# Second attention layer: the lead of a block's load and sum over its moments, and a buffer of the router's own for turned tokens

## The chip, the cores and the metric

The kernel runs on one core of a Trainium2 chip. The metric is the device time of one execution in microseconds (us). Times of the kernel before: 1226.37, 1233.04 and 1235.10 us, median 1233.04. The profile comes from one further execution.

## The reference, cut to what matters

Tokens x are 16 sequences of 256 with 128 features, 4096 tokens in all. Four residual sublayers follow each other: causal attention, a mixture of experts, a second attention with a distance-like score, and the same mixture of experts.

```python
x = x + attn_a(layernorm(x))   # 16 heads of 8, causal softmax
x = x + ffn(layernorm(x))      # 8 experts, each token goes to its best 2
x = x + attn_b(layernorm(x))   # softmax of -(|q|max^2 - 2 q k + |k|max^2) / (|q|_F * |x|_inf)
x = x + ffn(layernorm(x))      # the same weights

# ffn
logits = flat_x @ Wr
top_vals, top_idx = top_k(logits, 2);  rw = softmax(top_vals)
g = einsum('nc,ech->neh', flat_x, Wg); u = einsum('nc,ech->neh', flat_x, Wu)
eo = einsum('neh,ehc->nec', silu(g) * u, Wd) / sqrt(12)
out = sum over the two chosen experts of rw * eo
```

`layernorm` has no weights: (x - mean) / sqrt(variance + 1e-5), over the 128 features.

## The kernel before, in words

**Blocks and rounds.** The tokens are cut into 8 blocks (n = 0 to 7) of 512 tokens, which are two sequences (b = 0, 1). An attention layer runs 128 rounds, 16 for each block; each round handles two pairs of heads of one sequence. In a round PE makes scores by rows (`rows_scores`), DVE takes their maximum (`mx<-s`, `rows_maxima`), and 14 rounds later PE makes the scores of the same heads again by columns and ACT turns them into exponentials (`p<-s`). Three rounds after that PE multiplies them with the values (`av<-p,v`), and so on. Rounds of two blocks therefore overlap.

**The planner.** All other work of a layer is written as Python generators that yield between their steps `(rounds to wait, work(DVE us, ACT us, needs the PSUM bank))`. `later` (line 1306) puts a step on a list with the round from which it is due; `due` (line 1309), called twice in a round, takes the due steps in order of rank and age, as long as the DVE and ACT time stated for them fits the `room` of the round (1.7 and 1.4 us in the second layer) and the one PSUM bank `ps` (pool `mm`, one buffer) is not already claimed. `work()` without a number costs nothing in this account. The planner runs when the program is built; the engines then execute fixed queues, each in its order. All instructions of the kernel are recorded through one helper, so that nearly all show as line 250 in the profile; the names of tiles tell them apart. The scatters of the router are declared free of mutual order (`unordered`, line 471), and stand in POOL's queue earlier than the planner's round for them.

**The steps of a block.** `project(n)` (line 915) starts 15 to 17 rounds ahead of the block's own rounds in the second layer. It loads the block: in the second layer each token's value lies in DRAM as two halves, `xb` and `more` (line 898 to 913, on SP's DMA queue). Then, step by step: POOL adds the halves (line 925, `xb<-xb,more`); after a yield DVE takes the mean and variance (`moments`, line 316: `st<-xb`, `mv<-st`, two tiles of 128 tokens in one round and two in the next), POOL computes 1/sqrt and the shift (`rstd`, `shift`); ACT normalises into `xn` (line 336); PE transposes `xn` and ACT copies the result to `xnT` (`turned_block`, line 352); q and k are projected from `xnT`; scale factors are found from sums over q, k and x (`scales`, line 1050, with the small tile `den`, copied from PSUM by DVE and raised to a power by POOL); q is scaled and split into a high part by ACT and a low part by DVE (`hi`, `lo`, lines 980 to 991); the parts are laid out for the heads by DMAs on SP (`lay`, line 1019, `q<-hi`, `q<-lo`, `k<-hi`, `k<-lo`); last, the values are projected from the same `xnT` (line 994) and POOL adds a bias (`xb<-xb,extra_b`).

**The end of a block.** When a block's attention output `o` is complete, `finish(n)` (line 1272) is put on the list at line 1270: PE turns `o`, ACT copies it, PE projects it, DVE adds it to `xb`, and SP stores the sum. Then `route(n)` (line 376), the router: `moments` again, normalised rows into `both_rows` (ACT reads `xb` for the last time here, which frees the block's buffer; `blocks` has five of them, so the load of block n+5 waits for it), `turned_block` again, logits, the two best experts, the place of each token in its expert's queue, its two weights (DVE, `both_rows<-share`), and eight indirect DMAs on POOL that scatter the rows by expert (`rows_in<-both_rows,slots`).

**The experts.** Scattered rows form tiles of 256 (some of 128 in the second layer's end). A tile has four parts (`gu<-xT`, `y<-w_d,h`). One part can run in each round once tiles are known; what is left when the layer's loop ends runs alone after it (`rest`).

**Buffers.** A pool's `bufs` says how many tiles with one tag exist at a time. The attention's pool has two for each tag unless stated, and `xnT` of `project` and of `route` share one tag.

Of the kernel before, what the change touches and what calls it, by code (L numbers as in the profile page):

```python
# [45 lines left out]
F32 = mybir.dt.float32  # L46
# [8 lines left out]
P = 128  # L55
# [11 lines left out]
TB = 512  # L67
NT = TB // P
# [15 lines left out]
def work(v=0.0, s=0.0, bank=False):  # L84

    return bank, v, s
# [7 lines left out]
def layers(  # L94
# [73 lines left out]
    psum = ctx.enter_context(tc.tile_pool(name="mm", bufs=1, space=PSUM))  # L168
# [180 lines left out]
                ALU.subtract, ALU.mult,  # L349
            )  # L350

    def turned_block(pool, psum, xn, ts=range(NT)):

        ps = psum.tile([P, TB], F32, tag="mm")
        for t in ts:
            te.transpose(ps[:, bass.ts(t, P)], xn[:, t, :], ident)
        xnT = pool.tile([P, TB], F32, tag="xnT")
        some = slice(ts[0] * P, ts[-1] * P + P)
        se.copy(xnT[:, some], ps[:, some])
        return xnT  # L360
# [15 lines left out]
    def route(pool, psum, n, xb, free, mixture):  # L376

        mv, rstd, shift = yield from moments(pool, xb)  # L380
        yield 3, work(s=0.8)

        both_rows = pool.tile([P, 2, NT, W], F32, tag="both_rows", bufs=2)
        xn = both_rows[:, 0, :, 0:P]
        yield from normed_in_steps(xn, xb, rstd, shift)
        po.tensor_copy(
            both_rows[:, :, :, P],
            tokens[:, :, n * NT : (n + 1) * NT],
        )
        yield 2, work(s=0.6, bank=True)  # L390
        xnT = turned_block(pool, psum, xn)
        yield 1, work(s=0.6)
        se.copy(both_rows[:, 1, :, 0:P], xn)
        yield 1, work(0.8, bank=True)
        ps = psum.tile([P, NT, NE], F32, tag="mm")
        for t in range(NT):
            te.matmul(ps[:, t, :], lhsT=xnT[:, bass.ts(t, P)], rhs=wr_sb, start=True, stop=True)
        lg = pool.tile([P, NT, NE], F32, tag="lg")
        ve.tensor_copy(lg, ps)
        top1, one1 = yield from best(pool, lg, 1)  # L400
        yield 1, work(0.8)
        rest = pool.tile([P, NT, NE], F32, tag="rest")
        ve.scalar_tensor_tensor(rest, one1, -3.0e38, lg, ALU.mult, ALU.add)
        top2, one2 = yield from best(pool, rest, 2)
        both = chosen[n % 2]
        ve.tensor_tensor(both[:, 0:NT, :], one1, one2, ALU.add)
        share = pool.tile([P, 2, NT], F32, tag="share")
        ve.tensor_tensor(share[:, 1], top2, top1, ALU.subtract)
        yield 2, work(0.4, 0.2, True)
        se.activation(share[:, 1], share[:, 1], AF.Exp)  # L410


        ps = psum.tile([P, NT + 1, NE], F32, tag="mm")
        te.matmul(
            ps.rearrange("p t e -> p (t e)"), lhsT=before, rhs=both.rearrange("p t e -> p (t e)"),
            start=True, stop=False,
        )
        for t in range(NT):
            te.matmul(
                ps[:, t + 1 :, :], lhsT=ones_h,  # L420
                rhs=both[:, t : t + 1, :].to_broadcast([P, NT - t, NE]),
                start=False, stop=t == NT - 1,
            )
        place = pool.tile([P, NT, NE], F32, tag="place")
        ve.tensor_tensor(
            place, ps[:, 0:NT, :], free[0].unsqueeze(1).to_broadcast([P, NT, NE]), ALU.add
        )
        after = pool.tile([P, NE], F32, tag="after")
        ve.tensor_tensor(after, ps[:, NT, :], free[0], ALU.add)
        free[0] = after  # L430
        yield 1, work(0.9)
        row = pool.tile([P, 2, NT], F32, tag="row")
        for s, one in enumerate((one1, one2)):
            mine = pool.tile([P, NT, NE], F32, tag=f"mine{s}")
            ve.tensor_tensor(mine, one, place, ALU.mult)
            ve.tensor_reduce(row[:, s, :], mine, AX.X, ALU.add)
        ve.tensor_copy(slots[n], row)
        yield 1, work(0.6)

        w1, w2 = both_rows[:, 0, :, P + 1], both_rows[:, 1, :, P + 1]  # L440
        ve.tensor_scalar_add(share[:, 0], share[:, 1], 1.0)
        ve.reciprocal(share[:, 0], share[:, 0])
        ve.tensor_scalar_mul(w1, share[:, 0], DEPTH_SCALE)
        ve.tensor_tensor(w2, share[:, 1], w1, ALU.mult)
        last = n == TOKENS // TB - 1
        chosen_tiles = mixture.choose(n, free[0], last)
        if last:
            yield 1, work(0.9)
            yield from chosen_tiles
        for t in range(NT):  # L450
            for s in range(2):

                if s == 0 or not mixture.second:
                    yield 1, FREE
                scatter = po.indirect_dma_start(
                    out=rows_in,
                    out_offset=bass.IndirectOffsetOnAxis(ap=slots[n][:, s, t : t + 1], axis=0),
                    in_=both_rows[:, s, t, :], in_offset=None,
                )
                unordered(scatter, mixture.rows)  # L460
                mixture.sent.append(scatter)
                if last:
                    mixture.pad(2 * t + s)
        if not last and sure(n):
            yield 1, work(0.9)
            yield from chosen_tiles
        if sure(n):
            yield 2, FREE
            mixture.admit()
# [413 lines left out]
    def attention(w, causal, name, mixture, ahead=None):  # L883

        with ExitStack() as own:
            pool = own.enter_context(tc.tile_pool(name=f"att_{name}", bufs=2))
# [28 lines left out]
            def project(n, b0=0, nb=2):  # L915
# [4 lines left out]
                xb, ts = xs[n], range(2 * b0, 2 * (b0 + nb))  # L920
# [2 lines left out]
                yield (3, work(0.9)) if causal else (3 if n < 3 else 4, FREE)  # L923
                if not causal:
                    po.tensor_tensor(xb[:, ts[0] : ts[-1] + 1], xb[:, ts[0] : ts[-1] + 1], more, ALU.add)
                    yield 1 if n < 3 else 2, work(0.9)
                mv, rstd, shift = yield from moments(pool, xb, n < 2, ts, causal or n > 1)
                yield 3 if causal else 2, work(s=0.8)
                if causal and n == 0:
# [316 lines left out]
            def collect(n, b, f, av, o):  # L1246

                au = pool.tile([P, 2, SEQ], F32, tag="au")
                se.copy(au, av)
                yield 1, work(0.6, bank=True)  # L1250
                ps = mm[0].tile([P, 2, 2, 4, HS], F32, tag="mm")
                for t in range(2):
                    for e in range(2):
                        te.transpose(
                            ps[:, t, e, :, :].rearrange("p i r -> p (i r)"),
                            au[:, e, bass.ts(t, P)], ident,
                        )
                ps = ps.rearrange("p t e i r -> p t (e i) r")
                inv = pool.tile([P, 2, 8], F32, tag="inv")
                ve.reciprocal(inv, ps[:, :, :, 0])  # L1260
                width = 4 * HD
                ve.tensor_tensor(
                    o[:, 2 * b : 2 * b + 2, (f - 1) * width : (f + 1) * width].rearrange(
                        "p t (i r) -> p t i r", r=HD
                    ),
                    ps[:, :, :, 1 : 1 + HD],
                    inv.unsqueeze(3).to_broadcast([P, 2, 8, HD]), ALU.mult,
                )
                if b == 1 and f == NQ - 1:
                    later(2, work(s=0.6, bank=True), finish(n, outs.pop(n)))  # L1270

            def finish(n, o):
                ps = mm[0].tile([P, TB], F32, tag="mm")
                for t in range(NT):
                    te.transpose(ps[:, bass.ts(t, P)], o[:, t, :], ident)
                oT = pool.tile([P, TB], F32, tag="oT", bufs=1)
                se.copy(oT, ps)
                yield 1, work(0.7, bank=True)
                ps = mm[0].tile([P, NT, P], F32, tag="mm")
                for t in range(NT):  # L1280
                    te.matmul(
                        ps[:, t, :], lhsT=oT[:, bass.ts(t, P)], rhs=w["wo"], start=True, stop=True
                    )
                ve.tensor_tensor(xs[n], ps, xs[n], ALU.add)
                store = sy.dma_start(out=tokens_of(mixture.total, 0, n), in_=xs[n])
                unordered(store, mixture.adds)
                mixture.stores.append(store)
                yield 1, work(0.9)
                yield from route(pool, psum, n, xs.pop(n), free, mixture)
# [16 lines left out]
            def later(rounds_on, kind, task, rank=1):  # L1306
                tasks.append((at + rounds_on, kind, rank, task))
# [214 lines left out]
```

## Time and profile before

| What | Value |
|---|---|
| Runs | 1226.37, 1233.04, 1235.10 us |
| Profiled execution, its time / its span | 1236.46 / 1234.7 us |
| Mean granted TensorE clock | 0.924 |
| First layer's rounds | 24.9 to 378.4 us (first maximum to last exponential) |
| Its experts alone | about 404 to 580 us |
| Second layer's rounds | 580.9 to 1009.6 us |
| Its last routing and first tiles | to about 1091 us |
| Its experts alone, then the output | to 1206 us, to 1234.7 us |

The span runs from the first to the last instruction; the execution's own time is 1.8 us longer. Rows of a timeline give the start, the length, the engine, the operation and its tiles as out<-in; a bracket at the end tells how long the engine was idle before, and what ended that. A row of the waits names who waited for whom, the total, how often, and the longest. PE is TensorE's matrix engine and PEld its weight loads, DVE is VectorE, ACT is ScalarE, POOL is GpSimd, SP is the engine that issues most DMAs.

### The profile page before, as it was taken

The page shows a single profiled execution, that of the slowest core. Times are in us where ns is not written, and L with a number is a line of the kernel's source. Part 1 is how long each engine was busy: PE and PEld are TensorE (multiplying, and loading weights), DVE is VectorE, ACT ScalarE, POOL GpSimd, SP SyncE. Part 2 cuts the span into 40 slices and gives each one's busy share as a digit, 9 for nine tenths or more (in the row PEclk, how much of TensorE's full clock was granted, in tenths as well). Part 3 has the DMA queues.
Part 4 walks back from the last instruction along what each step waited for, and adds up shares of the span by engine and source line. Part 5 has one row for each costly group of instructions (what it writes and reads, how often), then busy time and mean ns, then how long its engine had stood idle before and what let it go on. Part 6 is the DMA issues. An engine that isn't in the chain of part 4 may idle for free. (4 is left out here: it accounts for less than half of the span.)

```text
span 1234.7 us, 24185 instructions
## 1 busy us (share of the span) xinstructions
PE 1015.7 (82%) x8128; PEld 740.9 (60%) x8128; DVE 804.8 (65%) x2289; ACT 631.3 (51%) x1331; POOL 601.7 (49%) x681
## 2 busy tenths in 40 slices
PE   5888888979988989996678788668888886889991
PEld 3455555646666879985344445435546665779980
DVE  6666887676754756665577867668687535656662
ACT  3466665535554434453246766556656663334440
POOL 5345666454576775565221220431516675555551
PEclk9899999989999999999569988888889999999996
DMA  3355433225335798775232222222243444678876
GB/s 98 85 152 151 115 89 104 79 69 166 76 96 118 184 210 196 176 193 111 69 88 75 58 70 62 80 83 71 74 134 84 108 96 125 162 186 210 219 173 212
DMA packets 185408, 151.49 MB, mean 123 GB/s; under 512 B 16322, under 2 KB 159940, under 8 KB 185284
## 3 DMA queue, kind: packets, MB, share of 16 engines
q1 hardware_dynamic: 155842, 127.18, 36.3%
q0 software_dynamic: 25552, 18.30, 10.0%
q10 hardware_dynamic: 3890, 4.46, 1.2%
q8 instruction: 65, 1.06, 0.4%
q14 instruction: 59, 0.48, 0.1%
HBM read 83.06 MB, written 32.08 MB: 93 GB/s over the span
## 5 line engine op out<-in xcount | busy, mean ns | idle before, releaser
L250 DVE TENSOR_REDUCE mx<-s 128x6 f32<-128x768 f32 (+1 forms) x256 | 276.7, 1087 | 84.9 <-PE s L250 74.7
L250 ACT ACTIVATE p<-s 128x768 f32<-128x768 f32 (+1 forms) x256 | 234.7, 917 | 170.5 <-PE s L250 155.0
L250 POOL DMA_INDIRECT total<-y,to x149 | 233.8, 1569 | 154.0 <-ACT sg L250 59.8
L250 DVE SCALAR_TENSOR_TENSOR sg<-sg,gu 128x256 f32<-128x256 f32 (+1 forms) x267 | 107.2, 401 | 148.8 <-ACT sg L250 91.8
L250 POOL DMA_INDIRECT rows_in<-both_rows,slots x128 | 127.8, 999 | 102.7 <-DVE both_rows L250 52.0
L250 PE MATMUL y<-w_d,h 128*128 128x128 f32 x1192 | 162.6, 279 | 17.4 <-ACT y L250 10.9
L250 PEld LDWEIGHTS y<-w_d,h 128*128 128x128 f32 x1192 | 156.2, 192 | 30.9 <-ACT y L250 14.3
L250 PE MATMUL gu<-xT,w_g 128*128 128x256 f32 (+1 forms) x534 | 158.9, 380 | 13.5 <-ACT xT L250 4.8
L250 ACT ACTIVATE sg<-gu 128x256 f32<-128x256 f32 (+1 forms) x267 | 98.7, 370 | 131.3 <-PE gu L250 86.0
L250 PE MATMUL gu<-xT,w_u 128*128 128x256 f32 (+1 forms) x534 | 153.9, 370 | 0.0
L250 PE MATMUL s<-k,q 62*128 62x256 f32 (+1 forms) x1024 | 137.8, 351 | 9.6 <-DVE mx L250 4.0
L250 POOL TENSOR_SCALAR_AFFINE_SELECT p<-p 128x512 f32<-128x512 f32 x128 | 88.3, 696 | 116.5 <-ACT p L250 116.0
L250 PE MATMUL s<-q,k 64*128 64x256 f32 (+1 forms) x1024 | 110.6, 296 | 30.7 <-DVE mx L250 25.6
L250 PE MATMUL av<-p,v 128*9 128x256 f32 (+1 forms) x2048 | 130.4, 374 | 0.0
L250 PEld LDWEIGHTS s<-k,q 62*128 62x128 f32 x1024 | 84.4, 204 | 74.3 <-issue 46.7
L250 PEld LDWEIGHTS s<-q,k 64*128 64x128 f32 x1024 | 83.6, 199 | 50.9 <-DVE mx L250 38.4
L250 PEld LDWEIGHTS gu<-xT,w_u 128*128 128x128 f32 x534 | 100.1, 193 | 12.5
L250 PEld LDWEIGHTS gu<-xT,w_g 128*128 128x128 f32 x534 | 87.6, 192 | 26.4 <-ACT xT L250 7.0
L250 DVE SCALAR_TENSOR_TENSOR h<-gu,sg 128x256 f32<-128x256 f32 (+1 forms) x237 | 95.8, 404 | 8.1
L250 ACT ACTIVATE y<-y,x_in 128x128 f32<-128x128 f32 x149 | 54.8, 368 | 79.1 <-PE y L250 57.5
L250 PEld LDWEIGHTS av<-p,v 128*9 128x9 f32 x2048 | 45.0, 92 | 65.5 <-issue 33.9
L250 POOL TENSOR_TENSOR lo<-to,hi 128x512 fp32r<-128x512 f32 (+1 forms) x27 | 32.3, 1195 | 78.3 <-ACT hi L250 77.1
(242 smaller groups left out, 1410.5 us busy)
## 6 DMA issues: line engine op xcount, KB each, us to landing
w_g<-in_L_ffn_Wg_dram SPq DMA_DIRECT2D x79, 256.0 KB
w_u<-in_L_ffn_Wu_dram SPq DMA_DIRECT2D x79, 256.0 KB
w_d<-in_L_ffn_Wd_dram SPq DMA_DIRECT2D x79, 256.0 KB
x_in<-rows_in SPq DMA_DIRECT2D x70, 130.0 KB
k<-hi SPq DMA_DIRECT2D x64, 128.0 KB
k<-lo SPq DMA_DIRECT2D x64, 128.0 KB
q<-hi SPq DMA_DIRECT2D x60, 128.0 KB
q<-lo SPq DMA_DIRECT2D x60, 128.0 KB
```

The costliest lines, as they stand in the source:

```text
L250: return tc.keep_in_program_order(method(*args, **kwargs))
```

## The change

Three things differ. First, in the second layer's `project`, for blocks 3 to 7, the yield between POOL's add and the moments is four rounds long, not two. Second, `turned_block` takes a tag and a number of buffers, and `route` calls it with a tag of its own, `routed`, with one buffer, so that the router's transposed tokens no longer share the two `xnT` buffers. Third, `finish` is put on the planner's list in both layers with an ACT time of 0 instead of 0.6 us; what it executes is the same.

```diff
-    def turned_block(pool, psum, xn, ts=range(NT)):
+    def turned_block(pool, psum, xn, ts=range(NT), tag="xnT", bufs=2):
...
-        xnT = pool.tile([P, TB], F32, tag="xnT")
+        xnT = pool.tile([P, TB], F32, tag=tag, bufs=bufs)
...
-        xnT = turned_block(pool, psum, xn)
+        xnT = turned_block(pool, psum, xn, tag="routed", bufs=1)
...
                     po.tensor_tensor(xb[:, ts[0] : ts[-1] + 1], xb[:, ts[0] : ts[-1] + 1], more, ALU.add)
-                    yield 1 if n < 3 else 2, work(0.9)
+                    yield 1 if n < 3 else 4, work(0.9)
...
                 if b == 1 and f == NQ - 1:
-                    later(2, work(s=0.6, bank=True), finish(n, outs.pop(n)))
+                    later(2, work(bank=True), finish(n, outs.pop(n)))
```

## The prediction, made before the changed kernel ran

> **What bounds the kernel now.** I read the page's head first, then the engines' busy time by stretch, then the second layer's waits, then a timeline where the longest wait lies, last the chain. The page:
>
> ```profile
> span 1234.7 us, 24185 instructions
> PE 1015.7 (82%) x8128; PEld 740.9 (60%) x8128; DVE 804.8 (65%) x2289; ACT 631.3 (51%) x1331; POOL 601.7 (49%) x681
> ```
>
> No engine is full over the whole. By stretch (length, then PE, PEld, DVE, ACT and POOL busy; PE clock):
>
> ```profile
> 640.00:728.00 88.00, 70.13 (x710) 39.95 (x710) 68.72 (x142) 65.41 (x116) 15.36 (x21) 0.98 0.23 64
> 728.00:832.00 104.00, 74.31 (x666) 44.24 (x658) 69.16 (x193) 59.80 (x108) 32.32 (x43) 0.86 0.26 72
> 1096.00:1205.00 109.00, 108.26 (x710) 98.35 (x708) 71.81 (x227) 50.84 (x154) 59.17 (x39) 1.00 0.80 196
> ```
>
> The last row is the second layer's expert tiles run alone: PE-bound, 99%. The two above are its attention rounds, and there PE, DVE and ACT are all under 80%: each round is a relay PE scores, DVE maximum, PE scores, ACT exponential, and a stop of one engine soon stops all. Between 728 and 832 PE drops from 80% to 71% busy. Its waits (total, times, longest, between 640 and 963):
>
> ```profile
> PE ps L250 <- DVE den L250: 18.9, 5, 7.5
> DVE st L250 <- POOL xb L250: 14.3, 3, 6.6
> POOL xb L250 <- DMA more<-total: 8.3, 1, 8.3
> SPq L250 <- ACT both_rows L250: 33.4, 3, 12.4
> ```
>
> The longest, in order of time (bracket: idle before, and what ended it):
>
> ```profile
> 820.92 0.17 DVE L250 TENSOR_TENSOR both_rows<-share,both_rows 128x4 f32<-128x4 f32 x1
> 821.18 1.08 POOL L250 DMA_INDIRECT rows_in<-both_rows,slots  x1 [17.56 <-DVE both_rows L250]
> ...
> 826.35 0.96 POOL L250 DMA_INDIRECT rows_in<-both_rows,slots  x1 [0.30 <-issue]
> 827.34 1.28 POOL L250 TENSOR_TENSOR xb<-xb,extra_b 128x512 f32<-128x512 f32 x1
> 828.56 1.27 POOL L250 TENSOR_TENSOR lo<-to,hi 128x512 fp32r<-128x512 f32 x1
> 829.78 1.26 POOL L250 TENSOR_TENSOR xb<-xb,more 128x512 f32<-128x512 f32 x1
> 831.07 0.29 DVE L250 BATCH_NORM_STATS2 st<-xb 128x6 f32<-128x128 f32 x1 [6.60 <-POOL xb L250]
> 831.97 0.15 DVE L250 COPY den<-ps 128x2 f32<-128x2 f32 x1
> 832.27 1.09 PE L250 MATMUL ps<-ident,o 128*128 128x128 f32 x4 [7.50 <-DVE den L250]
> 833.28 0.79 PE L250 MATMUL s<-k,q 62*128 62x256 f32 x4
> ```
>
> This is block 7's start. DVE finishes a router's weights at 820.92; only then POOL may start the router's scatters, which stand ahead of the block's add in POOL's queue; five scatters and two 1.3 us operations later the sum exists. DVE stood at the block's first statistic for 6.60 us; behind it waits `den<-ps`, which empties the one PSUM bank that PE's next transpose needs: PE stands for 7.50 us. Nothing works. The same picture stands at 782.97 (DVE 5.07, PE 5.98, block 6) and 730.69 (DVE 2.63, PE 3.54, block 5). Sums: DVE 14.3, PE 17.0 us.
>
> **The change part by part.** Nothing is computed that wasn't; it is a new order. I count rounds by DVE's 128 `mx<-s` of the layer.
>
> *Statistics four rounds after the add (line 926).* Block 7: before, the router's weights come in round 83 and the statistic in 85, with five scatters ahead of the add; after, 84 and 87, with six. POOL's path is then 6 x 1.26 + 1.26 = 8.8 us (1.26 is the step from one scatter to the next) against three rounds of 2.3 us (rounds 16 to 48, 642.5 to 717.4) to 3.0 us (48 to 96, to 863.5), 6.9 to 9: 0 to 1.9 us stay, I take 1.5; 5.1 go. Block 6: weights in round 67, statistic in 69 before; 61 and 71 after: all 5.07 go. The cover is POOL, free again by about round 65.
>
> Block 5's 2.63 has another cause: its load. The block takes the buffer of block 0, which the router reads in rounds 47 and 51, while the load stands in SP's queue in round 47: the SP row, 33.4 us in three waits, and POOL's 8.3 us for the landing. *`finish` with no ACT cost (line 1270)* lets the planner start it and the router sooner: the reads come in rounds 44 and 45 (blocks 6 and 7: 66/68 to 62/64 and 79/83 to 76/78, loads in 63 and 79). The 2.63 go. SP's freed time I cost at nothing: what stood behind it (scores' rows, k and q lays) was used rounds later.
>
> So DVE gets back 14.3 - 1.5 = 12.8 us. As nothing else ran, I count it whole. Is it more? After each stop DVE idles once more (2.00, 2.23, 2.00 us), while PE refills. Here a rule bears on it: the Trainium skill, "TensorE: Matmul & The Clock Gate", Part 1, halves the clock after an idle window of about 3.4 us and wants another of that length of work to restore it. The row agrees in kind (four `s` in 0.79 us after the stop, 0.50 at 822.28), not in size: by the rule three stops cost 3 x 3.4 / 2 = 5.1 us more; by the trace, 0.3 us per four matmuls and part of 6.2 us of idle. I take 2.
>
> *What comes later instead.* All later steps of a block move by four to five rounds, its q lay (four DMAs on SP) too: scaled in rounds 46, 61, 77, 93, 108 for blocks 3 to 7 (before 41, 57, 73, 89, 104), first used in 48, 64, 80, 96, 112. Rows for block 4:
>
> ```profile
> 759.37 1.22 DVE L250 TENSOR_REDUCE mx<-s 128x4 f32<-128x1024 f32 x1
> 763.13 0.50 PE L250 MATMUL s<-q,k 64*128 64x256 f32 x4 [0.23 <-DVE mx L250]
> ```
>
> These are round 61's maximum and round 64's scores. Scaled after it (0.89 us for the two `lo`), q is ready at 761.5; two issues and a landing follow. The DMA records of this trace give 2.0 us from the last issue to the last packet (issue 752.34, end 754.41), so q lands at 764.2, 1.1 us late; DVE's round-64 maximum began only at 766.14, so little is seen. Block 3 has two rounds: maximum at 713.11, q at 715.2, landed 717.9, scores wanted at about 715.4: 2.5 us. Behind PE's wait stand the values' matmuls and, by the bank, DVE. I take 2.5 + 3 x 0.5 = 4 us; between 0 (hidden) and 5 x 4 = 20 (landing as slow as the 7.26 us of the chain's `t<-total`).
>
> *The buffer of its own (lines 352, 391).* Needed since block n+1's turned tokens may now come before block n's are read out. No wait for an `xnT` buffer stands in the trace: 0, either way.
>
> *More tiles inside.* Routers end sooner (block 0's last scatter in round 65 instead of 71), so the layer's expert work starts in round 113 instead of 116: 68 parts instead of 64 lie inside the rounds, the loop has one turn more, and one tile less stays for the end. The chain prices a tile there:
>
> ```profile
> 1096.34 2.59 PE gu L250 x12
> 1101.80 2.59 PE gu L250 x12
> ```
>
> 5.5 us. The extra turn costs 2.4 (the last 34 run from 1009.6 to about 1091), the three parts in rounds 113 to 115 between 0 and 3 x 1.4; I take 1. Net -2.
>
> *The first layer* is reshuffled by the same `finish` line. Its turns (180) and parts inside (72) stay. A rule speaks here against counting on any order: the skill's "SBUF — State Buffer", "SBUF: two separate sides", says that GpSimd and a VectorE operation with two SBUF inputs lock each other out for whole instructions. The trace has it once dearly: `m<-mx`, usually 0.2 us, takes 4.98 at 255.20 beside four POOL operations, and PE idles 5.88 us. By the rule a new order can lift or repeat it: -5 to +5. By the rows, a dozen others cost 0.8 to 1.0 each: nearer 0, which I take.
>
> Sum: -12.8 - 2 + 4 - 2 + 0 = -13. The profiled execution took 1236.46 us (span 1234.7 and 1.8 around it), 3.4 over the median of 1233.04; -13 on either, so 1220 on the median's scale.
>
> **The rivals.**
> - *The stop moves* (0.24). One bank (`ps`), and a DVE in order, make any late operand a stop: six scatters before block 7's add, or another POOL operation behind them. For: POOL still gets scatters in runs of six. Against: blocks 5 and 6 have ten rounds of room. Half the gain, with q's 4: 1233 - 6.5 + 3, or less: 1226 to 1236.
> - *q comes late for every block* (0.14), the slower side. Place: PE at the first scores of blocks 3 to 7; it decides once q lands over two rounds, about 6 us, after the lo. At 6 us late for five blocks, 30 less the 17 gained otherwise, +13: 1246. For: SP also carries k's lay of the block's other half in the same round, four DMAs of 0.6 us. Against: 2.0 us landings in this stretch at 23 to 27% DMA share.
> - *More comes* (0.12): cold clock at the rule's 5 us, the 4.98 us lock gone, block 7's 1.5 too: 1209.
> - *Forecast* (0.50): 1213 to 1226.
>
> **How the numbers follow.** 1% is about what a measurement can tell from no change: 1220.7 and 1245.4. Faster by more: all of the 0.12 and about 0.29 of the forecast's 0.50, 0.41. Within 1%: 0.21 and 0.24, 0.45. Slower: 0.14. The range, 1207 to 1238, leaves out the late q and some of the best case.
>
> **What would show it.** DVE's waits for POOL's `xb` in the attention rounds under 4 us in all, PE's for `den` under 4; no SP wait for `both_rows` over 5 us; POOL's `xb` without a wait for `more`. A row "PE s <- DMA q" tells of late q: up to 4 us expected. The final tiles alone should take 5.5 us less. I am wrong if DVE's statistics run free and the layer's rounds still take as long, or if PE waits for q by more than 10 us.

## The result, and the profile after

The changed kernel takes 1239.15 us (median of 16 runs, 1233.45 to 1247.48) against 1232.32 us for the kernel before (16 runs): ratio 1.006, interval 1.0036 to 1.0084. Forecast was 1220 us. A few executions were slow ones, at a lower clock (two of seven in `three_rounds_blocks67`, at most two of 22 in the other runs): medians in this document are of all executions, ratios of the rest. The profiled execution took 1241.53 us, span 1239.7. Two lines of its page:

```profile
span 1239.7 us, 24203 instructions
PE 1033.8 (83%) x8128; PEld 752.7 (61%) x8128; DVE 797.4 (64%) x2286; ACT 635.4 (51%) x1334; POOL 602.4 (49%) x684
```

PE issues the same 8128 matmuls and is busy 18.1 us longer (1015.7 before). The same stretches as before the change, and the last expert tiles alone (length, then PE, PEld, DVE, ACT and POOL busy, PE clock, DMA share, GB/s):

```profile
640.00:728.00 88.00, 72.38 (x718) 42.04 (x716) 66.23 (x142) 64.08 (x114) 15.90 (x23) 0.94 0.25 68
728.00:832.00 104.00, 83.33 (x714) 48.11 (x706) 74.08 (x194) 62.79 (x113) 29.07 (x40) 0.84 0.25 70
1101.00:1210.00 109.00, 108.02 (x705) 97.92 (x705) 71.22 (x226) 50.00 (x151) 58.87 (x38) 1.00 0.83 202
```

Between 728 and 832 us PE now runs 80% of the time, not 71%, and 714 matmul records lie there instead of 666: this stretch did become faster. But the clock fell in both, from 0.98 to 0.94 and from 0.86 to 0.84. The waits of the rounds (640 to 975 us; total, times, longest):

```profile
POOL xb L250 <- DMA more<-total: 33.3, 3, 14.3
DVE mx L250 <- PE s L250: 31.6, 31, 4.0
DVE sg L250 <- ACT half_g L250: 13.0, 7, 4.9
ACT sg L250 <- POOL h L250: 4.2, 1, 4.2
PE s L250 <- DMA q<-lo: 1.8, 1, 1.8
PE ps L250 <- DVE den L250: 1.8, 2, 1.2
```

DVE's wait for POOL's sum (14.3 us) is gone from the list, PE's for `den` has fallen from 18.9 to 1.8, SP's for `both_rows` is gone too. POOL's wait for `more`, which was to go, grew from 8.3 to 33.3 us; no statistic of DVE waits behind it. What has grown is `mx` waiting for PE's scores (22.7 before) and DVE's `sg` waiting for `half_g` (5.1 before). Block 7's start, in order of time, shows how well the stop was removed:

```profile
830.33 1.27 POOL L250 TENSOR_TENSOR xb<-xb,more 128x512 f32<-128x512 f32 x1
831.54 1.27 POOL L250 TENSOR_TENSOR lo<-to,hi 128x512 fp32r<-128x512 f32 x1
832.98 0.98 POOL L250 DMA_INDIRECT rows_in<-both_rows,slots  x1 [0.17 <-issue]
...
833.46 0.29 DVE L250 BATCH_NORM_STATS2 st<-xb 128x6 f32<-128x128 f32 x1
```

Block 7's statistic begins at 833.46, in round 87 as the prediction had it, without a bracket: the sum (first line) had been ready for 1.86 us. In one profiled execution of each kernel, measured from one block's first maximum to the next one's, the stretches of 16 rounds went: rounds 48 to 95 together from 146.1 to 148.8 us although the three stops lay there, 96 to 111 from 51.5 to 57.4, 112 to 127 from 48.3 to 58.4; from the last maximum to the end 271.5 became 262.1.

### The profile page after: what moved, and what is told of

The parts are those of the page before. It is cut to its first block, busy times and chain, and to the rows that moved or that the text cites. A ratio compares the mean times of both kernels' runs of the same rounds, so it can differ in the third digit from the quotient of the medians.

```text
span 1239.7 us, 24203 instructions
## 1 busy us (share of the span) xinstructions
PE 1033.8 (83%) x8128; PEld 752.7 (61%) x8128; DVE 797.4 (64%) x2286; ACT 635.4 (51%) x1334; POOL 602.4 (49%) x684
## 5 line engine op out<-in xcount | busy, mean ns | idle before, releaser
L250 POOL DMA_INDIRECT total<-y,to x149 | 233.8, 1569 | 142.8 <-ACT sg L250 64.9
L250 POOL TENSOR_SCALAR_AFFINE_SELECT p<-p 128x512 f32<-128x512 f32 x128 | 85.5, 670 | 119.4 <-ACT p L250 118.4
L250 PE MATMUL av<-p,v 128*9 128x256 f32 (+1 forms) x2048 | 135.2, 383 | 1.7 <-POOL p L250 1.7
```

The costliest lines, as they stand in the source:

```text
L250: return tc.keep_in_program_order(method(*args, **kwargs))
```

## The experiments

The runs were made on five chips, on which the kernel before takes 1213 to 1232 us, so every ratio is to the kernel before on the same chip. Runs of one group share a chip.

| run | kernel before, us | this, us | ratio (95% interval) |
|---|---|---|---|
| `finish_only` | 1213.8 | 1225.2 | 1.0102 (1.0067 to 1.0137) |
| `finish_second_layer` | 1213.8 | 1221.0 | 1.0062 (1.0040 to 1.0083) |
| `add_early` | 1213.8 | 1224.8 | 1.0105 (1.0076 to 1.0133) |
| `first_layer_before` | 1213.8 | 1217.5 | 1.0027 (1.0011 to 1.0044) |
| `buffer_only` | 1224.3 | 1225.7 | 1.0006 (0.9985 to 1.0026) |
| `after_again` | 1224.3 | 1241.7 | 1.0144 (1.0113 to 1.0175) |
| `four_rounds_block7` | 1224.3 | 1240.0 | 1.0117 (1.0083 to 1.0151) |
| `three_rounds_blocks67` | 1224.3 | 1238.6 | 1.0098 (1.0060 to 1.0136) |
| `changed_parts_held` | 1213.3 | 1214.9 | 1.0023 (1.0002 to 1.0043) |
| `block7_parts_held` | 1213.3 | 1220.4 | 1.0052 (1.0033 to 1.0072) |
| `changed_h_on_dve` | 1213.3 | 1214.5 | 1.0007 (0.9991 to 1.0023) |
| `three_rounds_all` | 1213.3 | 1206.7 | 0.9944 (0.9921 to 0.9967) |
| `changed_with_parts` | 1232.0 | 1238.6 | 1.0061 (1.0042 to 1.0080) |
| `held_first_layer_before` | 1232.0 | 1247.3 | 1.0101 (1.0054 to 1.0147) |
| `three_rounds_first_before` | 1232.0 | 1237.9 | 1.0036 (1.0015 to 1.0057) |
| `three_rounds_h_on_dve` | 1232.0 | 1246.1 | 1.0103 (1.0062 to 1.0145) |
| `three_rounds_again` | 1231.2 | 1236.8 | 1.0035 (1.0016 to 1.0054) |
| `changed_same_chip` | 1231.2 | 1241.0 | 1.0071 (1.0047 to 1.0094) |

### The parts of the change, one by one

`finish_only` is the changed kernel with the yield after the add put back:

```
-                    yield 1 if n < 3 else 4, work(0.9)
+                    yield 1 if n < 3 else 2, work(0.9)
```

> The change without its four rounds: `finish` announced with no ACT cost (line 1270) and the routed buffer, the statistic still two rounds after the add. Three theories. Lateness (the four rounds push a block's k, q and scales into the last rounds before its first scores): this kernel has none of it, the stop of block 5 goes (2.63 us), blocks 6 and 7 keep theirs or lose them by the earlier router; 1222 to 1231 us. Finish (router and final projection pressed into earlier rounds cost ACT, PE and the one bank): this part alone costs, 1238 to 1250. Clock (with the stops gone PE's idle time is only spread, and the half clock is granted more often): as many stops as it loses, as much cold clock it wins, so 1229 to 1236, with cold time in the rounds between before's 61 us and after's 96.

1.0102, taken as a ratio in the range of the second theory: the `finish` line alone is a loss. `finish_second_layer` keeps it in the second layer only:

```
-                    later(2, work(bank=True), finish(n, outs.pop(n)))
+                    later(2, work(bank=True) if not causal else work(s=0.6, bank=True), finish(n, outs.pop(n)))
```

> As the run with `finish` alone, but only in the second layer; the first layer is before's. It prices the first layer's reshuffling: all theories expect the same second layer as in that run, and a first layer within 3 us of it (the profile of the changed kernel ends the first layer 2.2 us sooner), so 0 to 3 us slower than that run.

1.0062: faster than `finish_only`, where 0 to 3 us slower was expected. So of some 11.4 us about 7 come from the second layer and 4 from the first, which I had costed at nothing (the intervals of the two overlap; the next run repeats the first).

```
-                yield (3, work(0.9)) if causal else (3 if n < 3 else 4, FREE)
+                yield (3, work(0.9)) if causal else (3 if n < 3 else 2, FREE)
```

> The whole change, but the sum is put into POOL's queue two rounds after its load instead of four, so the statistic still comes four rounds after the sum and every later step of a block (k, scales, q) stands in the same round as in the kernel before. Lateness: the stops stay away and the late steps are gone, so the predicted gain comes out, 1215 to 1224 us. Clock: no stops, and still no gain, 1233 to 1242, with 85 us or more of cold clock in the rounds. Finish: 1236 to 1245, like the changed kernel. What could spoil it: POOL waits for the landing of the sum's second operand with its queue behind it (the profile of the changed kernel has 33 us of such waits that nobody saw).

This edit did not do what it says: every engine's order of instructions came out as in `finish_only`, since nothing of POOL stands between the two places. The expectation tells nothing, but the same order measured twice gave 1.0102 and 1.0105.

`first_layer_before` is `finish_second_layer` with the four rounds, which is the changed kernel but for the first layer:

```
-                    yield 1 if n < 3 else 2, work(0.9)
+                    yield 1 if n < 3 else 4, work(0.9)
```

> The whole change with the first layer as before (`finish` at no ACT cost only in the second). The second layer should take what it takes in the changed kernel, the first 2.2 us more by the profile: 1239 to 1244 us under all theories. If it is faster than the changed kernel by more than 3 us, the first layer's order is part of the cause and the profile of one execution misled.

1.0027. (The expected microseconds are the first chip's; the changed kernel itself did not run on this one.) This gives the pair that carries the study: it differs from `finish_second_layer` in the four rounds alone, on one chip. The four rounds bring 3.5 us (about 1 to 6, when the executions of both are resampled). The views of the two, over rounds 16 to 111, first with two rounds (`finish_second_layer`):

```profile
629.70:896.80 267.10, 212.50 (x1960) 126.40 (x1960) 197.22 (x511) 173.48 (x314) 72.64 (x98) 0.90 0.27 72
```
```profile
DVE mx L250 <- PE s L250: 16.8, 19, 1.6
DVE st L250 <- POOL xb L250: 11.9, 3, 5.1
```

and with four (`first_layer_before`):

```profile
633.40:903.50 270.10, 220.27 (x1960) 130.64 (x1960) 204.35 (x519) 176.79 (x315) 73.74 (x98) 0.88 0.27 72
```
```profile
DVE mx L250 <- PE s L250: 28.3, 29, 2.5
PE s L250 <- DMA q<-lo: 1.8, 1, 1.8
```

The stops (11.9 us) are gone, and these rounds are no shorter: 270.1 us, against 267.1 here and 266.5 and 269.7 in `finish_only` and `add_early`, whose second layer has the same order with two rounds. (Each is one execution. In those of the pair the time up to the second layer's first maximum differs by 4.9 us, though the first layer is the same in both kernels, so 3.0 us more is not a loss shown.) Where the stops lay, in rounds 48 to 95, 3.4 us are gained; rounds 16 to 47 lose 0.9 and rounds 96 to 111 lose 5.6. What the kernel gains comes at the end: 260.8 us from the last maximum, against 268.0, 267.0 and 267.4.

Two things took the place of the stops. PE's 1960 matmuls are the same and take 7.8 us longer, and DVE waits 11.5 us more for the scores: PE stands at half its clock for 64.9 us of these rounds instead of 51.2. Over all executions of the two kernels, the median of the mean granted clock is 0.919 with four rounds and 0.926 with two. And DVE itself is busy for 204.4 us instead of 197.2. Three single instructions account for that much. They take 7.2 us more than others of their kind: `spread<-ident,term` at 749.80 (1.96 us, usually 0.23), `parts<-m,parts` at 820.61 (3.17, usually 0.19), and `share<-top`, usually 0.15, here in DVE's and POOL's rows:

```profile
885.49 2.60 DVE L250 TENSOR_TENSOR share<-top 128x4 f32<-128x4 f32 x1
886.20 1.85 POOL L250 TENSOR_TENSOR xb<-xb,extra_b 128x512 f32<-128x512 f32 x1
888.01 1.21 DVE L250 TENSOR_REDUCE mx<-s 128x4 f32<-128x1024 f32 x1
```

Each of the three ends within 0.06 us of a POOL operation on 128x512 elements that ran beside it. It is the pattern of the 4.98 us that the prediction found in the first layer. In `finish_second_layer` nothing of the kind exceeds its usual length by more than 0.8 us in these rounds. With four rounds in every block it came back in all eight profiles, on five chips or more, in rounds 62, 87 and 106 (2.0, 1.4 to 3.2 and 2.5 to 2.6 us, in round 87 often, and in round 106 once, on another DVE instruction); with three rounds it is absent from those places. That POOL's operation is the cause was not tested by moving it.

Why is PE's clock lower? In `first_layer_before` its four longest spells of half clock between rounds 16 and 96 begin in rounds 40, 56, 74 and 87, about where a block's statistic meets a router's. In the planner's order for `finish_second_layer` the second halves of these stand at rounds 38 and 42, 54 and 58, 70 and 74, 86 and 90 (the statistics of blocks 4 to 7, and of the routers of blocks 0 to 3; in the kernel before at the same rounds, or two more apart). With four rounds they stand at 40 and 40, 57 and 58, 73 and 72, 89 and 88, and so in the changed kernel. Two windows of `first_layer_before`, in rounds 39 to 40 and 55 to 56, each with what follows:

```profile
684.40:687.80 3.40, 1.91 (x23) 0.99 (x23) 3.19 (x13) 1.94 (x4) 0.10 (x1) 1.00 0.03 8
687.80:698.10 10.30, 9.38 (x65) 5.31 (x57) 6.94 (x15) 5.56 (x9) 5.49 (x11) 0.50 0.01 3
```
```profile
728.80:732.20 3.40, 1.64 (x22) 0.76 (x22) 3.17 (x12) 1.18 (x2) 0.00 (x0) 1.00 0.00 0
732.20:742.40 10.20, 8.95 (x56) 4.80 (x52) 7.17 (x22) 3.25 (x7) 4.09 (x9) 0.50 0.01 3
```

DVE (third busy figure) works 3.2 of 3.4 us, PE only 1.9 and 1.6; then the clock stands at 0.50 for 10 us. DVE's queue inside the first window, in order of time:

```profile
684.79 0.29 DVE L250 BATCH_NORM_STATS2 st<-xb 128x6 f32<-128x128 f32 x1
685.12 0.18 DVE L250 BATCH_NORM_AGGREGATE mv<-st 128x2 f32<-128x6 f32 x1
685.22 0.26 DVE L250 BATCH_NORM_STATS2 st<-xb 128x6 f32<-128x128 f32 x1
685.51 0.18 DVE L250 BATCH_NORM_AGGREGATE mv<-st 128x2 f32<-128x6 f32 x1
685.61 1.19 DVE L250 TENSOR_REDUCE mx<-s 128x4 f32<-128x1024 f32 x1
686.72 0.28 DVE L250 BATCH_NORM_STATS2 st<-xb 128x6 f32<-128x128 f32 x1
```

The statistics stand between one maximum and the next, and PE's next scores wait for the maximum. These here are both of block 4; the router's stand at 681.98 and 687.53, just before the window and at its end. Over 630 to 960 us the half clock is granted for 75 us in this run and for 58 in `finish_second_layer`, where its long spells come with the stops instead. Two long spells follow directly on long DVE instructions: the one of round 87 (13.7 us from 824.35, after 3.40 us in which PE was busy 0.76), and 10.2 us from 889.21 (after 1.14 of 3.40). So whether the meeting of the statistics or the long instructions lower the clock is open; a kernel that keeps the statistics apart with all else equal was not tried, and `four_rounds_block7` below loses time although they stand four rounds apart in it. Nor were four rounds in every block without the `finish` line: in that order the engines wait for one another in a circle.

### One stop alone, beside the buffer alone

`buffer_only` has the new buffer and nothing else; `after_again` is the changed kernel on that chip.

> The kernel before with the routed buffer alone: the order of instructions on every engine is before's, only an address differs. 0 us, ratio 0.998 to 1.002, under all theories; its profile is before's on this chip.

> The changed kernel beside its parts on one chip: 1.004 to 1.009 by the first measurement. If `finish` is the cost (1.010 alone with the four rounds left out, 1.006 with them, on two chips), it lies here below 1.010 again; if the earlier ratio was the chip's, at 1.010.

1.0006 and 1.0144: the buffer costs nothing, and the change costs more than on its first chip, so the second expectation's bound was passed. `four_rounds_block7` takes away only the longest stop, with `finish` as before:

```
-                    yield 1 if n < 3 else 2, work(0.9)
+                    yield 1 if n < 3 else 2 if n < 7 else 4, work(0.9)
```

> The kernel before, with four rounds from sum to statistic in block 7 alone, and `finish` as before: DVE's longest stop (6.60 us, PE 7.50) should go and nothing else of the change is there. Finish theory: stops are worth what they cost, so 4 to 7 us faster (ratio 0.994 to 0.997). Clock theory: the idle time comes back spread, 0 to 2 us. Lateness: block 7's later steps come later too, -3 to +3.

> The kernel before, with three rounds from sum to statistic in blocks 6 and 7, and `finish` as before. One round of 2.3 to 3 us more for each: by the prediction's sum 2.6 us of block 6's 5.07 and 2.6 of block 7's 6.60 go, so 5 us faster (0.994 to 0.998); by the clock or the lateness theory -1 to +3 us.

(The second has `2 if n < 6 else 3`.) Both missed by much: 1.0117 and 1.0098. In the first, block 7's stop is gone, and rounds 80 to 95 take 3.0 us less than in `buffer_only` (48.5 against 51.5); rounds 96 to 127 take 18.5 us more (114.1 against 95.6), of which 3.1 come back at the end. (The profiled execution was 5 us above its kernel's median.) In rounds 96 to 127 ACT waits 9.6 us for POOL's `h`, in `buffer_only` not at all. Removing 6.6 us of standing made the kernel 14 us slower than `buffer_only`: what a later statistic pushes into later rounds can cost twice what the stop did. Which of the steps that moved costs it was not tried.

### Expert parts and POOL's queue

From these runs I formed another theory: the loss lies in rounds 112 to 127, where the second run of expert parts now begins in round 113 instead of 116, and the parts' product `h` stands in POOL's queue behind the router's scatters. The changed kernel (POOL, then what waited before it):

```profile
924.52 0.96 POOL L250 DMA_INDIRECT rows_in<-both_rows,slots  x1 [0.30 <-issue]
925.78 0.96 POOL L250 DMA_INDIRECT rows_in<-both_rows,slots  x1 [0.30 <-issue]
926.77 0.75 POOL L250 TENSOR_TENSOR h<-half_g,sg 128x256 f32<-128x256 f32 x1
```

Six scatters begin at 919.36, when the router's rows are ready, and the first `h` comes behind them. `changed_parts_held` holds the parts back to round 116:

```
-            if self.now is None and self.loaded and "xT" in self.loaded[0]:
+            if self.now is None and self.loaded and "xT" in self.loaded[0] and not (self.second and 104 <= at < 116):
```

> The changed kernel, with the second layer's second run of expert parts held back to round 116, where it stood before the change (there it begins in round 113). Crowding theory: the rounds' loss sits where three parts start beside the router's six scatters, whose POOL queue their product `h` stands in; rounds 112 to 127 fall from 57 us to about 48 (before: 47.2), rounds 96 to 111 stay at 57, and the end takes 6 to 9 us more than the changed kernel's 261: 0 to 4 us faster than the changed kernel, ratio 1.008 to 1.013. Clock theory: rounds 112 to 127 stay above 54, and the end is still longer, so slower than the changed kernel, 1.017 or more.

> Four rounds in block 7 alone (1.0117), with the second run of expert parts held from round 113 to round 116. Crowding: rounds 112 to 127 fall from 57 to about 48 us, the end rises by 3 (267 to 270), so 5 to 7 us faster than that run: 1.005 to 1.008; what then is left lies in rounds 96 to 111 (56.9 against 48.4 before). Clock or lateness of block 7: no fall, 1.012 or more.

(The second does it to `four_rounds_block7`, from round 107.) 1.0023, under the figures given, and 1.0052. In the first, rounds 112 to 127 took 44.6 us and the end 269.7, as crowding has it, but rounds 96 to 111 took 52.6, not 57.

Two more runs of the group: `h` on DVE in the second layer's rounds, and three rounds from sum to statistic in every block (`else 3` in place of `else 4`, the rest of the change kept).

```
-            self.second = self.relieved = name == "b"
+            self.second, self.relieved = name == "b", False
```

> The changed kernel, with the expert parts' product `h` on DVE inside the second layer's rounds too (as the first layer has it) instead of POOL. Crowding behind POOL's scatters: the waits of ACT for POOL's `h` (4 to 5 us) and most of DVE's for `half_g` go, DVE gets 20 parts of some 0.4 us more; rounds 112 to 127 fall by 4 to 8 us, 1.008 to 1.012. If POOL's queue is not the place (the parts are only too many for PE or the one bank), 1.014 to 1.020.

> The changed kernel with three rounds instead of four. By the planner the second run of expert parts then begins in round 117 (before the change 116, with it 113). Crowding: rounds 112 to 127 take 46 to 50 us, and the end 270 or more; block 7's stop is gone or under 4 us; 1.002 to 1.010. Finish theory (its earlier router is the cost whatever the parts do): 1.010 to 1.015. Lateness: a quarter to a half less than the changed kernel's loss.

1.0007 and 0.9944, both under the figures given: with three rounds instead of four the kernel beat the one before on this chip, by 6.6 us. I took all four for the theory. But the end of `three_rounds_all` took 261.7 us, not 270 or more, and the changed kernel itself had not been run on this chip. The next four runs put it beside kernels of this kind on one of the slower chips:

> The changed kernel, on one chip with the three runs below: 1.006 to 1.0145, as on the two chips before.

> The changed kernel with the second run of expert parts held to round 116 and the first layer as before. Crowding: the parts' early start is worth 3 to 6 us and the first layer 2 to 5 (1.0144 and 1.0027, 1.010 and 1.006 on other chips), so 5 to 11 us faster than the changed kernel here, ratio 0.996 to 1.002. If the first layer's order costs nothing, 1.001 to 1.004.

> Three rounds instead of four, and the first layer as before. Three rounds alone gave 0.9944. If the first layer's order costs 2 to 5 us, 0.990 to 0.993; if it costs nothing, 0.993 to 0.996.

> As the run before, and the product `h` on DVE in the second layer's rounds. In the changed kernel this took 4 to 8 us off because the parts stood behind POOL's scatters; here they begin in round 117, after most scatters, so -2 to +3 us against the run before: 0.990 to 0.996. If it gains 4 us or more, POOL's queue holds the parts up even at their late start.

Here the theory fell as an account of the whole loss. With the parts held and the first layer as before, 1.0101 against 1.0061: rounds 112 to 127 fell from 58.3 to 53.0 us, but the end rose from 262.2 to 272.5. What the early parts cost inside (5.3 us) they more than save at the end (10.3). `h` on DVE made the three-round kernel 8 us slower. Three rounds with the first layer as before lost to the kernel before, 1.0036. The last pair asked for three and four rounds on one chip:

> Three rounds instead of four, again. If its gain is the order's, 0.992 to 0.998 here too. If it was the chip's (chips whose kernel before takes 1213 us lose less to a late operand than those at 1224 to 1232), 0.994 to 0.998 on a chip of 1213 us, 1.000 to 1.008 on one of 1224 or more.

> The changed kernel beside the run above: 1.006 to 1.0145 if its loss is the order's on every chip; on a chip of 1213 us 1.000 to 1.004 if the loss depends on the chip (there its second layer with before's first one gave 1.0027). In all cases 5 us or more slower than three rounds, by the later start of the expert parts and of a block's late steps there.

1.0035 against 1.0071: three rounds beat four by 4.3 us, a little under what was expected, and lose to the kernel before. The 0.9944 belonged to its chip as well as to its order. One kernel on two chips, `three_rounds_all` and then `three_rounds_again`, rounds 112 to 127:

```profile
897.20:944.00 46.80, 41.45 (x363) 27.82 (x360) 32.28 (x86) 29.26 (x55) 20.53 (x26) 0.93 0.43 123
```
```profile
916.70:971.40 54.70, 47.81 (x364) 31.31 (x362) 32.12 (x86) 29.38 (x56) 21.18 (x27) 0.78 0.37 106
```

DVE, ACT and POOL are busy as long on both; PE needs 6.4 us more for the same matmuls, at 0.78 of its clock instead of 0.93, and the rounds take 7.9 us more. But the second profile is of the slowest of its 22 executions (1244.5 us, mean clock 0.904). Over all executions the median clock is 0.920 and 0.916, and within each kernel 0.01 of clock goes with some 6 to 11 us. So by this estimate the clock explains 3 to 5 of the 30 us between the chips, and the rest is open.

## Why the prediction was wrong

- **The stops go: right.** All three, and SP's wait for `both_rows`, as "What would show it" asked; POOL's wait for `more` grew instead of going. The sentence on being wrong came true as well: the statistics run free, and the layer's rounds take as long.
- **"As nothing else ran, I count it whole", 12.8 us: the step that failed.** In the pair on one chip 11.9 us of stops went, the rounds from 16 to 111 were no shorter, and the median fell by 3.5. In place of the stops DVE's own work took 7.1 us more (three instructions, beside POOL's operations, 7.2), and PE's same matmuls 7.8 us more. I priced only q's lay among "all later steps", and allowed for DVE held up beside POOL in the first layer alone; the statistic is a later step itself, on DVE, and the steps behind it came to stand beside others. That the engines were slower is shown; what made each slower is read from traces.
- **The cold clock, -2: wrong sign.** I followed the half clock only where the stops were. The rule I weighed (the Trainium skill, "TensorE: Matmul & The Clock Gate", Part 1) gave 5.1 us for the three stops and would have made the change look better still. The trace has the opposite: 7.8 us more for the same 1960 matmuls. The half clock came also after a window in which PE was idle only in pieces, the longest 1.1 us, at round 40.
- **q laid later, +4: right in kind, 1.8 measured**, at block 3 as named. The rival of q late for every block did not come.
- **`finish` removes block 5's stop, 2.63: not by itself.** With `finish` alone DVE's waits for the sum are still 11.9 us, three of them, block 5's still 1.78. The line by itself costs 7 us in the second layer. In `finish_second_layer` these lie in rounds 112 to 127, 54.5 us against 47.2 in `buffer_only` (another chip), with DVE's `sg` waiting 13.8 us for `half_g` and ACT 6.0 for POOL's `h`, against 1.1 and none. (The trace of `buffer_only` lacks some records of what ended a wait; all of DVE's waits before `sg` in it come to 4.0 us.)
- **More tiles inside, -2: both terms too small.** The end fell by 9.5 us, not 5.5, and rounds 112 to 127 grew by 10.1, not 3.4 (one execution each). Together about nothing, near the -2 by luck.
- **The buffer, 0: right** (1.0006, interval 0.9985 to 1.0026).
- **The first layer, 0: about +4 on one chip** (uncertain by as much), inside its bound of 5; with three rounds, on two slower chips, 1.0035 and 1.0036 show no difference. The single profile of the changed kernel had it 2.2 us shorter (the second layer's first maximum at 578.73 us, before 580.94): one execution does not settle such a size.

Of the rivals, "the stop moves" was nearest, but what came in its place was PE's clock, DVE's own instructions and `h`, not block 7's sum, and its 1226 to 1236 still took part of the gain as sure. Open are: what each meeting of two statistics and each long DVE instruction costs by itself, why `finish` costs less where the four rounds are added, and why the chips differ.

## What to carry to other kernels

In a chain where engines hand work to each other every 2 to 3 us, don't book a removed stop at its length: write down where each step behind it lands, on the engine that sets the pace, and what already stands in those rounds. Compare the busy time of each engine, and the longest of each kind of instruction, before and after: a list of waits doesn't show an instruction that was itself held up. Look at the clock row of the windows around those places as closely as at the waits, since 10 us at half clock can follow a window that is half empty in pieces as they follow a long stop. And compare parts of a change on one chip only; the kernels with three and with four rounds stood 1.2% apart on two chips (0.9944 and 1.0061), and 0.36% on one.

## What the runs showed of the hardware

PE's half clock needed no long pause. In `first_layer_before` the window 684.4 to 687.8 us has PE busy 1.91 of 3.40 us, with no pause over 1.1 us, and the next 10.3 us ran at 0.50.

A short DVE instruction can take more than ten times its usual time beside a POOL operation: 2.60 us instead of 0.15 in the rows shown above, ending 0.04 us after POOL's.

The same kernel took 1206.7 us on one chip and 1236.8 on another, while the kernel before differed by 18 us between them. The clocks of 0.93 and 0.78 in the two windows shown above are of one execution each, the second an extreme one.
